# An adaptive-layernorm block on one core: the last four groups of tokens go through every expert, and the end is scheduled anew

## The chip, the core and the metric

The kernel runs on one NeuronCore of a Trainium2 chip. The metric is the device time of one execution in microseconds (us). The engines are TensorE (PE; its weight loads are listed apart as PEld), VectorE (DVE), ScalarE (ACT), GpSimd (POOL) and SyncE (SP), which here issues nearly all DMAs. Each engine works through its own list in order.

## The reference

Eight sequences `x` of 2048 tokens and 256 channels go through one block; all arithmetic is float32:

- six vectors per sequence (shift, scale and gate for each half) come from `silu(c) @ wmod`; the gates are kept away from zero;
- `h = layernorm(x) * (1 + ca) + sa`, then linear attention with 16 heads of 64 channels: queries and keys through `elu + 1`, a decay per token and head `a = sigmoid(h @ Wa + ba + 2)`, a running state `S = a S + k v^T` and a running sum `z = a z + k`, output `(q S) / (q z + eps)`, then `@ Wo`; `x = x + ga * that`;
- `h = layernorm(x) * (1 + cb) + sb`, then a mixture of 8 experts, each a 256 x 256 matrix with a bias: softmax of `h @ gate_W + gate_b`, the best two experts with their weights (at least 0.1 each, then scaled to a sum of one), `out = sum(weight * (h @ W_e + b_e)) / 2`; `x = x + gb * out`.

## The kernel before

**Groups and steps.** The tokens are cut into 64 groups of 256 (two chunks of 128), eight groups to a sequence. One loop over `n` from -2 to 64 (L1180) writes out the work of all engines by hand: in step `n` group `n` does its attention (`c0` and `c1`, the two chunks: scores, keys, values, outputs, state, project), group `n+1` its projections to queries and keys, running sums and denominators, group `n+2` its first norm and decays, group `n-1` (`prev`) its second norm and its routing. Generators (`routing`, `norm`, `project`, `chunk_decays`, ...) are moved on piece by piece by `advance`, so the order in the loop body is the order of each engine's list. Step 64 has no group of its own, only the norm and the routing of group 63; behind it comes a loop for what is left, the tail.

**Routed experts.** The groups of one unit (`UNITS`, L59: one sequence; the last sequence has a unit of four groups and one of two) scatter their normed rows, as they are routed, into a list per expert in DRAM (`xrows`, one indirect DMA of POOL for each chunk and choice). When the unit's last group is routed, `plan` turns the counts into a table of tiles of 128 rows. An `ExpertTile` then loads its rows `xg` and its expert's weights `we` (SP reads row and expert from the table into registers first), `turn`s the rows (two PE transposes, two ScalarE operations that apply shift and scale to `xgT`), and `apply`s them (four PE records `py`, one DVE sum with the bias, one store to `yrows`). At most four such tiles are on the chip (`AHEAD`), at most two turned. When all tiles of a unit are done, a `Combine` for each of its groups gathers the two results of every token (four indirect DMAs of POOL into `yc`), loads `x` again (`xc`, one buffer), weighs and adds (ScalarE, then DVE, then a multiply by the gate and an addition, L1032 and L1033), and stores.

**How many tiles where.** `share` holds five numbers for a step: so many tiles at its start, behind the second norm's transposes (L1260), behind the decays of the coming group (L1310), behind chunk 1's scores (L1346) and at its end (L1393). `expert_tiles(k, look)` turns one tile ahead of the one it applies; with `look` false the last one turns nothing ahead. In the last sequence (`late`, from step 57) the shares are `[1, 3, 3, 3, 2]`, `[0, 0, 0, 3, 2]` where a new unit has only been planned, and `[3, 2, 1, 0, 3]` in step 63.

**Dense experts.** The last two groups (`dense_from = total - 2`) are not scattered. All eight experts are applied to all their tokens: a `DenseTile` is one expert on one group, eight PE records that take the group's `h2T` as it stands and two DVE sums (L973) that weigh the product by `comb`, the matrix of weights with zeros for experts not chosen. The expert matrices are put over the query and key weights `wq_sb` and `wk_sb` once no projection is left, that is in step 63 (L1266 to L1275). `biases` (L917) starts the sums `acc`: `comb` is turned on PE, copied by DVE, multiplied by the biases on PE, copied by ScalarE. `finish` (L937) multiplies by the gate and adds to `xt` on DVE, then stores.

**The end.** Combines are fetched and finished once in the middle of a late step (L1291 to L1293) and once at its end (L1385, L1398). From step 64 on, three buffers that are free by then (`rooms`: dec, kT, qT) hold a whole combine each; those multiply and add on DVE, the others on POOL. In step 64 routed and dense tiles are mixed one by one (L1188 to L1194).

**Queues.** What a DMA on SP waits for holds everything behind it on SP: each routed tile puts a store, two register loads and two loads there, and the denominators (`rdd`, L474, then `rb`, L479), the decays (`dec` L419, `el` L409), the combines' `xc` and their stores stand in the same list. Indirect DMAs stand in POOL's list with its arithmetic.

## Time and profile before

| | |
|---|---|
| median of 14 runs | 3657.91 us (3651.53 to 3670.09) |
| profiled execution | 3657.18 us, span from first to last instruction 3655.5 us |
| granted TensorE clock, mean | 0.985 |
| PE busy | 3467.5 us, 95% of the span |
| DVE, ACT, POOL busy | 2760.2, 2068.4, 1897.0 us |
| chain that ended last | PE 64%, DVE 19%, DMA 7%, ACT 4% |
| DMA | 712.11 MB, mean 195 GB/s |
| routed tiles | 311 (`we` loads) |
| gathers and scatters | 248 gathers for 62 combines, 248 + 72 scatters |

The page's strip divides the span into 40 slices and gives the busy share of each engine in tenths; the windows view gives busy time, granted clock and DMA share in a stretch that one names; the waits view lists who waited for whom; the timeline has the instructions in order. A routed tile shows as four records of L900 (`py`) behind two of L884 (`pxt`), a dense one as eight of L966 (`py_d`).

### The profile page before, as it was taken

To read this page: it belongs to the slowest core of one execution; us is meant where nothing else is said; L and a number is where in the kernel's file an instruction comes from. 1 tells how busy PE (TensorE), PEld (TensorE's weight loads), DVE (VectorE), ACT (ScalarE), POOL (GpSimd) and SP (SyncE) were. 2 spreads that over 40 slices of the span, in tenths; PEclk is the share of its full clock that TensorE was granted. 3 is DMA by queue.
4 is the path that set the end of the run, shared out by engine and by line. 5 is a ranking of instruction groups with operands and counts; after the bars stand their busy time and mean duration, and the time that the engine had idled before them with its cause. 6 is when DMAs were issued, how large, how long until landed. Compare 5 with 4: busy or idle time off the path is not lost.

```text
span 3655.5 us, 82235 instructions
## 1 busy us (share of the span) xinstructions
PE 3467.5 (95%) x28998; PEld 2676.3 (73%) x28998; DVE 2760.2 (76%) x6395; ACT 2068.4 (57%) x5295; POOL 1897.0 (52%) x2114
## 2 busy tenths in 40 slices
PE   8999999999999999999999999999999999989886
PEld 6777767777777777777777777777777777666665
DVE  5777787887787777787777778777788777767755
ACT  5555555565566565566556555556656556555532
POOL 3444453443655556555565556555465555555654
PEclk9999999999999999999999999999999999999988
DMA  6555447656667767767776766766766776777866
GB/s 171 148 161 149 127 147 203 182 168 189 194 194 216 210 178 218 206 193 205 196 209 197 226 189 186 232 182 195 222 186 197 222 197 182 226 215 225 235 210 206
DMA packets 347406, 712.11 MB, mean 195 GB/s; under 512 B 43736, under 2 KB 212968, under 8 KB 322416
## 3 DMA queue, kind: packets, MB, share of 16 engines
q1 hardware_dynamic: 318880, 631.29, 60.9%
q0 software_dynamic: 27264, 74.49, 6.0%
q8 instruction: 229, 3.75, 0.4%
q14 instruction: 185, 1.52, 0.1%
q10 hardware_dynamic: 848, 1.07, 0.1%
HBM read 577.29 MB, written 132.53 MB: 194 GB/s over the span
## 4 chain that ended last, share of the span: by engine, by line
PE 64%; DVE 19%; DMA 7%; ACT 4%; issue 3%; SPq 1%; POOL 1%; DVEq 0%; POOLq 0%; ACTq 0%
PE pv L542 11%; PE pw L629 9%; PE pk L340 9%; PE po L579 6%; PE pq L340 6%; PE py L900 6%; DVE at L447 5%; PE sc L506 4%; PE po L562 3%; DMA rb<-rdd 3%; PE ps L613 3%; DVE qT L352 2%; PE pxt L884 2%; PE pk L525 2%; DVE dec L515 2%
## 5 line engine op out<-in xcount | busy, mean ns | idle before, releaser
L429 ACT ACTIVATE dec<-dec,lt 128x128 f32<-128x128 f32 x2048 | 628.7, 389 | 20.3 <-POOL dec L423 20.2
L1177 POOL TENSOR_TENSOR at<-at,qT 128x512 f32<-128x512 f32 x256 | 341.8, 1347 | 414.0 <-DVE qT L352 334.3
L542 PE MATMUL pv<-wv_sb,hT_a 128*128 128x512 f32 x1024 | 487.9, 609 | 25.7 <-DVE kd L528 23.1
L340 PE MATMUL pk<-hT_a,wk_sb 128*128 128x256 f32 x2048 | 503.3, 391 | 0.0
L340 PE MATMUL pq<-hT_a,wq_sb 128*128 128x256 f32 x2048 | 485.4, 385 | 2.3 <-DVE yg L904 1.2
L629 PE MATMUL pw<-wo_sb,oT 128*128 128x256 f32 x2048 | 470.1, 383 | 6.3 <-DMA el<-led 4.7
L889 ACT ACTIVATE xgT<-pxt,modT,modT 128x128 f32<-128x128 f32 x622 | 247.3, 448 | 393.1 <-PE pxt L884 392.6
L629 PEld LDWEIGHTS pw<-wo_sb,oT 128*128 128x128 f32 x2048 | 387.5, 192 | 58.0 <-DVE oT L591 7.6
L340 PEld LDWEIGHTS pk<-hT_a,wk_sb 128*128 128x128 f32 x2048 | 377.6, 194 | 59.6 <-DVE dx L633 6.7
L340 PEld LDWEIGHTS pq<-hT_a,wq_sb 128*128 128x128 f32 x2048 | 379.1, 190 | 55.5 <-ACT xgT L889 2.2
L447 DVE TENSOR_TENSOR_SCAN at<-at,z,kT 128x256 f32<-128x256 f32 x448 | 406.8, 948 | 2.0
L423 POOL TENSOR_SCALAR_AFFINE_SELECT dec<-dec 128x2048 f32<-128x2048 f32 x128 | 261.9, 2046 | 272.8 <-DMA dec<-led 159.3
L515 DVE TENSOR_TENSOR dec<-sc,dec 128x512 f32<-128x512 f32 x512 | 326.9, 681 | 42.3 <-PE sc L506 42.3
L900 PE MATMUL py<-we,xgT 128*128 128x256 f32 x1244 | 339.6, 398 | 17.7 <-ACT xgT L889 8.3
L542 PEld LDWEIGHTS pv<-wv_sb,hT_a 128*128 128x128 f32 x1024 | 186.1, 192 | 226.9 <-issue 164.8
L591 DVE TENSOR_TENSOR oT<-po,rb 128x512 f32<-128x512 f32 x256 | 168.7, 685 | 206.9 <-DMA rb<-rdd 114.4
L506 PE MATMUL sc<-qT,kT 64*128 64x128 f32 x4096 | 295.7, 284 | 0.0
L634 POOL TENSOR_TENSOR xt<-xt,dx 128x256 f32<-128x256 f32 x128 | 93.5, 730 | 388.0 <-DVE dx L633 386.1
L506 PEld LDWEIGHTS sc<-qT,kT 64*128 64x128 f32 x4096 | 248.3, 187 | 62.3 <-issue 62.3
L350 ACT ACTIVATE lowq<-pq 128x512 f32<-128x512 f32 x256 | 152.8, 597 | 246.7 <-PE pq L340 146.2
L1062 POOL TENSOR_TENSOR el<-el,qT 128x1024 f32<-128x1024 f32 x120 | 287.1, 2392 | 5.6 <-POOL whole L1070 0.2
L549 ACT COPY v<-pv 128x512 f32<-128x512 f32 x256 | 146.9, 580 | 252.8 <-PE pv L542 252.8
(198 smaller groups left out, 6269.3 us busy)
## 6 DMA issues: line engine op xcount, KB each, us to landing
dec<-led SPq DMA_DIRECT2D x128, 1024.0 KB
we<-ew_d SPq DMA_DIRECT2D x311, 384.0 KB
at<-ad SPq DMA_DIRECT2D x128, 512.0 KB
el<-led SPq DMA_DIRECT2D x256, 256.0 KB
rb<-rdd SPq DMA_DIRECT2D x128, 512.0 KB
xg<-xrows SPq DMA_DIRECT2D x311, 128.0 KB
yrows<-yg SPq DMA_DIRECT2D x311, 128.0 KB
xt<-in_L_attn_x_dram SPq DMA_DIRECT2D x64, 256.0 KB
```

Of the source, the lines that this page charges most:

```text
L340: nc.tensor.matmul(pp[:, j * GT : (j + 1) * GT], w[:, k, (jj + j) * P : (jj + j + 1) * P], hT[:, k, :], start=(k == 0), stop=(k == KD - 1),)
L423: nc.gpsimd.affine_select(out=dec, in_=dec, compare_op=ALU.is_ge, fill=1e30, base=0, pattern=[[0, H], [1, C]], channel_multiplier=-1,)
L429: nc.scalar.activation(dec[:, h, :], dec[:, h, :], AF.Exp, scale=-1.0, bias=x.lt[:, 0, ch, h : h + 1])
L447: nc.vector.tensor_tensor_scan(zz[:, j, :], at[:, j, :], kT[:, j, :], 0.0 if z is None else z[:, j : j + 1], ALU.mult, ALU.add,)
L506: nc.tensor.matmul(sc[q][:, i, :], self.kT[rows, half * 4 + i, self.tok], self.qT[rows, half * 4 + i, self.tok], start=True, stop=True,)
L515: nc.vector.tensor_mul(w4, sc[q], w4)
L542: nc.tensor.matmul(pv, self.hT[:, k, self.tok], wv_sb[:, k, i * 512 : (i + 1) * 512], start=(k == 0), stop=(k == KD - 1),)
L629: nc.tensor.matmul(pw[:, :D], self.oT[:, j, :], wo_sb[:, j, :], start=(j == 0), stop=(j == NP - 1))
L889: nc.scalar.activation(self.xT[:, k, :], pt[:, k * P : (k + 1) * P], AF.Identity, bias=modT[3][:, k, b : b + 1], scale=modT[4][:, k, b : b ...
L900: nc.tensor.matmul(py[:, :D], self.xT[:, k, :], self.w[:, k, :], start=(k == 0), stop=(k == KD - 1))
L1062: nc.gpsimd.tensor_mul(el, el, x.qT[:, :, ch * C : (ch + 1) * C])
L1177: nc.gpsimd.tensor_mul(zz[:, part, :], zz[:, part, :], ahead.qT[:, part, :])
```

## The change

- The unit of the last sequence's groups 4 and 5 is dropped, and `dense_from` becomes `total - 4`: groups 60 to 63 are dense. `h2T` gets four buffers, `comb` too; the sums of four groups fill the tile that held those of two and the biases' matrix, so that matrix moves to a buffer of its own.
- Since the expert matrices can be loaded only in step 63, the dense groups are collected (`dense_units`) and started by `start_dense`: two in the middle of step 63, where the load of the table of tiles stood, the third ahead of that step's last share, the fourth in the middle of step 64. `biases` is cut in two, `turn_weights` and `biases`, and leaves `routing`; for several groups all are turned first.
- The late shares become `[1, 3, 1, 3, 3]`, in step 63 `[1, 3, 3, 3, 3]` and in step 64 `[5, 2, 3, 3, 2]`, with the first of step 64 behind the second norm's first half and two single tiles between the pieces of the last routing. In late steps the turn ahead of the third share is left out, and that share's last tile turns nothing ahead.
- From step 61 a third combine is finished and fetched in each step, behind the fourth share (`finish_outputs`, `fetch_outputs(False)`, a further `fetch_x`).
- All combines multiply and add on GpSimd. In the tail a combine is finished when four tiles have passed since it was fetched (`age`).

```diff
@@ -56,7 +56,7 @@
     NG = N // GT
 
 
-    UNITS = [(b, 0, NG) for b in range(B - 1)] + [(B - 1, 0, NG - 4), (B - 1, NG - 4, NG - 2)]
+    UNITS = [(b, 0, NG) for b in range(B - 1)] + [(B - 1, 0, NG - 4)]
 
     def tiles_of(unit):
         return (TOP_K * GT * (unit[2] - unit[1]) + E * (P - 1)) // P
@@ -316,7 +316,7 @@
                     ident,
                 )
         hT = wk2.tile(
-            [P, KD, GT], F32, tag=f"hT{shift}", name=f"hT_{tag}", bufs=2 if shift else 3
+            [P, KD, GT], F32, tag=f"hT{shift}", name=f"hT_{tag}", bufs=4 if shift else 3
         )
         for half in range(KD):
             nc.scalar.activation(
@@ -693,10 +693,6 @@
             nc.vector.tensor_mul(comb, picks[:, :, 0, :], wide(top[:, :, 0:1]))
             nc.vector.tensor_mul(mark, picks[:, :, 1, :], wide(top[:, :, 1:2]))
             nc.vector.tensor_add(comb, comb, mark)
-            yield
-            yield
-            yield
-            unit.biases()
             yield
             return
 
@@ -912,21 +908,27 @@
 
         def __init__(self, x):
             self.x, self.n = x, f"d{x.tag}"
-            self.comb = wk2.tile([P, G, E], F32, tag="comb", name=f"comb_{x.tag}")
-
-        def biases(self):
-
+            self.comb = wk2.tile([P, G, E], F32, tag="comb", name=f"comb_{x.tag}", bufs=4)
+
+        def turn_weights(self):
             pt = small_tile(f"pct_{self.n}")
             for ch in range(G):
                 nc.tensor.transpose(pt[:E, ch * P : (ch + 1) * P], self.comb[:, ch, :], ident)
-            turned = wk2.tile([P, GT], F32, tag="rd", name=f"combT_{self.n}", bufs=1)
-            nc.vector.tensor_copy(turned[:E], pt[:E, :GT])
+            part = self.x.n - dense_from
+            self.turned = wk2.tile(
+                [P, GT], F32, tag=("rd", "lnn")[part > 0], name=f"combT_{self.n}", bufs=(1, 6)[part > 0]
+            )
+            nc.vector.tensor_copy(self.turned[:E], pt[:E, :GT])
+
+        def biases(self):
+
+            turned = self.turned
             pb = small_tile(f"pb_{self.n}")
             for ch in range(G):
                 nc.tensor.matmul(
                     pb[:, ch * D : (ch + 1) * D],
                     turned[:E, ch * P : (ch + 1) * P],
-                    sums[:E, 2 * G, :],
+                    expert_b_sb[:E, :D],
                     start=True,
                     stop=True,
                 )
@@ -988,7 +990,8 @@
         def load(self, room=None):
 
             u = self.unit
-            self.engine = nc.vector if room else nc.gpsimd
+            self.room, self.age = room, 0
+            self.engine = nc.gpsimd
             if room:
                 hold = wk2.tile([P, 4 * TOP_K, D], F32, tag=room, name=f"xyc_{self.tag}")
                 self.x = hold[:, G * TOP_K : G * TOP_K + G, :]
@@ -1081,7 +1084,8 @@
     for n, (b, first, end) in enumerate(UNITS):
         for g in range(first, end):
             unit_of[b * NG + g] = n
-    dense_from = total - 2
+    dense_from = total - 4
+    dense_units = []
     def rest(gen):
 
         for got in gen:
@@ -1162,7 +1166,7 @@
             no_x.pop(0).load_x()
 
     def finish_outputs():
-        while len(fetched) > (2 if rooms else 0):
+        while fetched and len(fetched) > (2 if fetched[0].room else 0):
             fetched.pop(0).finish()
 
     def keep_sums(jj):
@@ -1175,6 +1179,16 @@
         if ahead:
             part = slice(2 * jj, 2 * jj + 2)
             nc.gpsimd.tensor_mul(zz[:, part, :], zz[:, part, :], ahead.qT[:, part, :])
+
+    def start_dense(some):
+
+        for u in some:
+            u.turn_weights()
+        for u in some:
+            u.biases()
+            queue.extend(DenseTile(u, e) for e in range(E))
+            left[u.n] = E
+            dense_units.remove(u)
 
     c0 = plan = planned = None
     for n in range(-2, total + 1):
@@ -1195,7 +1209,7 @@
 
         todo = len(queue) + len(loaded) + len(turned)
         if late and (todo or not planned):
-            share = [1, 3, 3, 3, 2]
+            share = [1, 3, 1, 3, 3] if here else [5, 2, 3, 3, 2]
         elif planned:
             share = [0, 0, 0, 3, 2] if late else [0, 0, 0, 2, 2]
         else:
@@ -1204,16 +1218,19 @@
                 -(-todo * (i + 1) // (5 * steps)) + (-todo * i // (5 * steps)) for i in range(5)
             ]
         if n == total - 1:
-            share = [3, 2, 1, 0, 3]
+            share = [1,3,3,3,3]
         own = here.dk if here else None
         if here:
             c0.scores(0)
             c0.keys()
             c0.scores(1)
-        expert_tiles(share[0], not late or n == total)
+        if here:
+            expert_tiles(share[0], not late)
         if prev:
             nf = norm(prev.xt, "f", prev.tag)
         advance(nf, 2)
+        if not here:
+            expert_tiles(share[0])
         if here:
             c0.values(0)
             c0.values(1)
@@ -1259,11 +1276,12 @@
         fetch_x()
         expert_tiles(share[1])
         if prev:
-            if n - 1 == dense_from:
+            if n == total - 1:
 
                 sums = wk2.tile([P, NP, GT], F32, tag="at", name="sums", bufs=1)
-                nc.sync.dma_start(out=sums[:E, 2 * G, :], in_=expert_b)
-            if n - 1 == dense_from:
+                expert_b_sb = wk2.tile([P, 2 * GT], F32, tag="low", name="expert_b_sb", bufs=2)
+                nc.sync.dma_start(out=expert_b_sb[:E, :D], in_=expert_b)
+            if n == total - 1:
 
                 for e in range(0, E, 4):
                     for k in range(KD):
@@ -1275,6 +1293,7 @@
                         )
             if n - 1 >= dense_from:
                 unit = DenseUnit(prev)
+                dense_units.append(unit)
             else:
                 u = unit_of[n - 1]
                 if units[u] is None:
@@ -1284,7 +1303,11 @@
         advance(rt)
         if coming:
             coming.hT = modulated(arows, coming.b, 0, 1, f"a{coming.tag}")
+        if n == total:
+            expert_tiles(1)
         advance(rt)
+        if n == total:
+            expert_tiles(1)
         advance(own, 2)
         if here:
             c0.project()
@@ -1296,7 +1319,7 @@
         advance(da)
         advance(zk)
         advance(kp)
-        if share[2]:
+        if share[2] and not late:
             turn_tile()
         advance(kp)
         advance(rt)
@@ -1307,7 +1330,7 @@
         if n == -1:
             gate_rows()
             gates_of[0] = gates(0)
-        expert_tiles(share[2])
+        expert_tiles(share[2], not late or not here)
         advance(dk)
         advance(zk)
         if ahead:
@@ -1333,9 +1356,8 @@
             planned = None
             for _ in range(AHEAD):
                 load_tile()
-        if prev and unit.dense:
-            queue.extend(DenseTile(unit, e) for e in range(E))
-            left[unit.n] = E
+        if n >= total - 1:
+            start_dense(dense_units[:2])
         advance(dk, 2)
         fetch_x()
         if here:
@@ -1344,6 +1366,9 @@
             c1.scores(1)
         advance(rt)
         expert_tiles(share[3])
+        if n > dense_from:
+            finish_outputs()
+            fetch_outputs(False)
         advance(dk)
         if not here:
             if ahead:
@@ -1368,6 +1393,7 @@
         advance(rt)
         advance(na)
         advance(dk)
+        fetch_x()
         if ahead:
             whole_decay(ahead, 0)
             decayed_queries(ahead, 0)
@@ -1390,6 +1416,8 @@
                 gates_of[ahead.b], f"{ahead.tag}_0",
             )
             c0.decay_state()
+        if n >= total - 1:
+            start_dense(dense_units[:])
         expert_tiles(share[4])
         if na is not None:
             arows = next(na)
@@ -1416,7 +1444,11 @@
     fetch_x()
     while queue or loaded or turned:
         expert_tiles(1)
-        finish_outputs()
+
+        for o in fetched:
+            o.age += 1
+        if fetched and fetched[0].age > 3:
+            fetched.pop(0).finish()
         fetch_outputs()
     while waiting or fetched:
         fetch_outputs()
```

## The prediction

> **What bounds the kernel now.** I read the page first, then busy time by step, then what TensorE (PE) waits for in the last steps, then the last 15 us in order of time. A step's end is taken at its second dx (L633), the last vector operation of chunk 1.
>
> From the page:
> ```profile
> PE 3467.5 (95%) x28998; PEld 2676.3 (73%) x28998; DVE 2760.2 (76%) x6395; ACT 2068.4 (57%) x5295; POOL 1897.0 (52%) x2114
> ...
> PE   8999999999999999999999999999999999989886
> ```
> PE is the bound except in the last four slices. The same by step: 54 (an ordinary one), then 57 to 63, then 64 with the tail (columns: PE, weight loads, DVE, ACT, POOL, granted clock, DMA share, GB/s).
> ```profile
> 2949.00:3002.80 53.80, 52.97 (x462) 41.28 (x462) 40.73 (x97) 32.47 (x83) 29.33 (x33) 1.00 0.71 204
> 3107.50:3169.10 61.60, 55.54 (x464) 42.61 (x466) 49.82 (x115) 32.93 (x85) 39.64 (x50) 0.97 0.68 201
> 3169.10:3240.00 70.90, 64.27 (x504) 48.72 (x504) 47.91 (x106) 38.48 (x99) 37.00 (x41) 0.98 0.80 233
> 3240.00:3313.40 73.40, 64.88 (x504) 49.39 (x504) 48.35 (x105) 38.70 (x99) 36.56 (x41) 0.95 0.81 225
> 3313.40:3380.70 67.30, 60.08 (x493) 45.79 (x494) 48.69 (x107) 36.20 (x93) 36.17 (x39) 1.00 0.79 224
> 3380.70:3442.60 61.90, 55.85 (x464) 42.61 (x464) 45.65 (x108) 32.69 (x83) 48.71 (x59) 0.97 0.73 211
> 3442.60:3509.30 66.70, 60.87 (x492) 46.84 (x492) 45.67 (x95) 34.70 (x87) 37.83 (x40) 1.00 0.82 247
> 3509.30:3572.10 62.80, 47.76 (x352) 36.25 (x352) 27.16 (x82) 18.60 (x50) 28.40 (x37) 0.81 0.64 193
> 3572.10:3655.50 83.40, 50.52 (x216) 40.06 (x216) 50.98 (x137) 20.21 (x48) 38.82 (x41) 0.84 0.70 216
> ```
> An ordinary step leaves PE idle 0.8 us, steps 57 to 62 six to nine each, step 63 15.0, the last stretch 32.9 at a clock of 0.84. What PE waits for in steps 58 to 62, and in step 63:
> ```profile
> PE pxt L884 <- DMA xg<-xrows: 18.9, 13, 4.9
> ```
> ```profile
> PE pxt L884 <- DMA xg<-xrows: 8.9, 1, 8.9
> PE py L900 <- ACT xgT L889: 3.0, 2, 2.6
> PE pb_d L926 <- DVE combT_d L923: 2.9, 1, 2.9
> ```
> Expert rows that have not landed. All engines' waits from 3572 on, first and second longest, then the timeline's last dense tiles and last operation:
> ```profile
> ACT xyc L1028 <- DMA xyc<-yrows,rows: 24.8, 10, 5.6
> POOL yc L1032 <- DMA we<-ew_d: 17.5, 1, 17.5
> ```
> ```profile
> 3637.47 7.17 PE L966 MATMUL py_d<-wk_sb,hT_f 128*128 128x256 f32 x32 [1.41 <-DVE sums L973]
> ...
> 3651.59 0.42 DVE L1033 TENSOR_TENSOR xyc<-xyc 128x256 f32<-128x256 f32 x1
> ```
> ScalarE waits for gathers, turns expert tiles late, and PE waits for those; behind PE's last matmul (3644.6) come 11 us of combining.
>
> **Unit prices.** A dense tile is 8 records: 7.17/4 = 1.79 us of PE. Two routed tiles lie between 3503.45 (first transpose) and 3505.68 (next project): 1.1 us each, but also two register loads and three DMAs on SP (3.6 us a tile without waits: xg issued at 3495.4, 3499.0, 3502.7). A gather costs POOL 1.26 us from start to start.
>
> **The balance.** Removed: 15 routed tiles (16.5 us PE, 54 us of SP), two combines (8 gathers), the ranks, plan and 16 scatters of the ninth unit. Added: 16 dense tiles (28.6 us PE) and two more bias sets (transposes 0.38, matmuls 1.13: 3.0 together). PE gets 15 us more work, so any gain must come out of waits. All 32 dense tiles must run after step 63 has overwritten the query and key weights.
>
> **Tiles by step**, counted from the shares. Before, steps 57 to 63: 5, 12, 12, 10, 5, 12, 9 routed, then 12 routed and 16 dense. After: 5, 11, 11, 11, 1+6, 11, then 6 routed and 6 dense (3+3), then 17 dense (shares 5, 2, 3, 3, 2 and two singles), and 9 in the tail. Steps 57 to 62 hold 56 tiles either way.
>
> **Steps 57 to 62.** The share after the decays falls from 3 to 1, without its turn ahead, and the last share rises from 2 to 3.
> - Gone: the waits at that place, 3.14 (3198.7), 4.89 (3269.9), 2.54 (3343.8) and 0.88 us (3471.6): 11.5. Half-clock stretches of 3.4 and 6.8 us follow the first two; half of them is lost, some 4.5 where PE works. In step 61, with group 60 dense, prank's wait for hist (1.47) and one behind qT (1.13) go: 2.6. Together 18.5.
> - Added: no turned tile is left for the fourth share; where that is so now (3150.0, 3423.6) PE waits 1.40 and 1.23 for ScalarE. Four steps by 1.3: 5.2. The third tile of the last share needs a load issued some 3 us earlier; loads take 2.4 to 8.5 us from issue to PE's release here, so 0 to 3 a step, middle 1.5: 6.
> - A third combine a step from 61: one more finish (ACT 2 x 0.49, DVE 2 x 0.48, POOL 2 x (0.89 + 0.72), one store and one load on SP) and four gathers, 5.0 us of POOL, in place of 5.1 us of scatters that dense groups lack. Its finish follows some 10 us behind its gathers, which take 5.0 and land 2.7 to 8.9 us after issue. ScalarE queues in order: behind its wait stand the last share's turns, then PE; DVE's sums stand behind ScalarE. Steps 61 and 62, 0 to 4.5 each with clock: 6. The store waits for POOL on SP ahead of rdd, but rdd now goes 3.7 us after rd; inside that I cost it nothing; uncovered, it delays rb by the same.
> - Sum 17.2 - 18.5 = -1.3, from -13 (only the 5.2 is paid) to +15 (11.5 gained; 5.2, 12 and 9 paid).
>
> **Step 63.** Three routed tiles fewer (-3.3), six dense (+10.7), two bias sets (+3.0). The first share falls from 3 to 1, so the 8.9 us wait goes, with 1.7 of half clock. Dense weights, 2 MB issued at 3540.5, are used now only at 3584; soon they are needed some 12 us after issue. At this step's 193 GB/s they take 10.9: wait 0 to 5, take 1. Sums behind an unlanded gather: 0 to 3, take 1. The combT wait stays. Sum +1.8, from -3 to +8.
>
> **Step 64 and the tail.** No DMA feeds PE here any more.
> - PE: 26 x 1.79 = 46.5; norm's transposes 1.2, gate 1.0, bias 1.5: 50.2.
> - Waits. Norm's second half stands on DVE behind the sums of five dense tiles: 0.5 + four small operations 0.8 + ACT 1.1 + handovers 0.3 = 2.7 (now 3.6). combT 0.6 to 2.9: 1.2. Matmuls behind DVE's sums 0 to 4.3 (now 4.3 with eight combines on DVE): 1.5.
> - Clock. Gaps of 2.40 (3127.1) and 1.80 us (3400.3) were followed by 3.4 us at 0.50; one of 2.54 (3343.8) was not. Two stretches: 0 to 6, take 3.
> - End: last matmul 3644.64 to last store of the dense finish 3646.78, and 3.46 from the last store to the end of the span: 5.6.
> - Combines: backlog gone, four left (before: nine in this stretch). POOL's sums are finished three to five tiles ahead of the end: nothing. Uncovered, 3.2 us on POOL against 1.7 on DVE for the last one.
> - Sum 64.2 against 83.4: -19.2, from -27 (all waits zero) to -11.
>
> **Two rules set against rows.** The Trainium skill, "GPSIMD Engine Reference", section Key points, says that VectorE is about twice as fast in elementwise work, which speaks against the move of the sums. The rows agree (multiply 0.89 and 0.42 us), and paid in full on three combines it would make the sum 4.5 us worse; the cover decides. "TensorE: Matmul & The Clock Gate", section What's actually happening, lets the clock fall after at least one idle window of about 3.4 us. By it none of my waits would cost clock, and the sum would be 3 us better; the rows after 1.80 and 2.40 decide against it.
>
> **Forecast.** The profiled execution is 3657.2 us with a span of 3655.5; the median, 3657.9, differs by less than the runs do among themselves. 3657.2 - 1.3 + 1.8 - 19.2 = 3638.5; I say 3638.
>
> **Rivals.**
> - *The spreading pays in full and the end closes tight*: -13, -1, -24: 3619. For it: the waits for rows are the largest item of PE in these steps. Against: no more than four tiles are on chip either way, so a wait may only move.
> - *The late steps take it back*: +10 and +6 against -19: 3654. For it: ScalarE and DVE queue in order behind gathers in steps 61 to 63. Against: only three steps.
> - *Dense sums or weights bound the end*: DVE has 52 sums by 0.48 = 25 us, norm and routing 7, finishes 6.8, combines 3.8, 43 of 64 us in order; if its pieces fall badly the gain is 7: 3650.
> - *Slower: SP's queue behind rb.* The third tile of the last share puts yrows, xg and we behind rb, where each tile holds SP for 5.7 to 8.3 us (yrows at 3242.2, 3250.5, 3256.2), ahead of the next chunk's dec and el. If steps 58 to 63 lengthen by 7 each, 42 - 19: 3680. It decides from (19 + 7)/6 = 4.4 us a step. Against: POOL's mask waits only 1.9 us for dec over steps 58 to 60.
>
> **Chances.** Forecast 0.50, spreading in full 0.22, taken back 0.12, end bound 0.08, SP 0.08. About 0.2% (7.3 us) is what can be told from no change. Faster takes in the first two, half of the end's case and a sixth of the third: 0.78; same 0.14; slower 0.08. The likeliest case alone reaches from 3626 to 3650; for eight in ten the range goes from the first rival's 3616 (its 3619 with the clock's 3) to 3656.
>
> **What would show it.** Right: the last stretch about 64 us with dense matmuls nearly without gaps, no waits for xg at the third share, last operation a dense xt add. Wrong: PE waits for xgT behind yc in steps 61 and 62; dense matmuls waiting for wq_sb; combines after the last matmul. The forecast fails if steps 57 to 63 change by more than 12 us in sum, or if the clock of the last stretch stays at 0.84.

## The result, and the profile after

The changed kernel takes 3692.04 us (median of 9 runs, 3684.16 to 3697.36) against 3658.47 us for the kernel before (43 runs, 3646.5 to 3671.78): a ratio of 1.0088, 95% interval 1.0075 to 1.0100. It is 33.6 us slower, where 20 us faster was forecast. Its profiled execution took 3702.28 us with a span of 3700.6; the granted clock is 0.982.

From the page of the changed kernel, busy time and PE's strip in 40 slices:

```profile
PE 3496.1 (94%) x29038; PEld 2700.0 (73%) x29038; DVE 2771.5 (75%) x6355; ACT 2053.5 (55%) x5263; POOL 1887.7 (51%) x2098
...
PE   8999999999999999999999999999999999887788
```

The last slice is better than before (8 for 6), but of the five ahead of it two are at 7 and three at 8, where two were at 9 and three at 8. By step, cut at the second dx as in the prediction: 57 to 63, then step 64 with the tail (columns: PE, weight loads, DVE, ACT, POOL, granted clock, DMA share, GB/s).

```profile
3121.50:3182.90 61.40, 56.55 (x464) 43.53 (x466) 50.15 (x115) 33.03 (x85) 39.66 (x50) 0.94 0.68 200
3182.90:3252.20 69.30, 62.24 (x498) 47.94 (x499) 47.94 (x105) 37.84 (x97) 36.98 (x41) 0.98 0.82 235
3252.20:3329.00 76.80, 64.00 (x498) 50.38 (x498) 45.80 (x104) 37.40 (x97) 36.54 (x40) 0.93 0.70 197
3329.00:3409.30 80.30, 65.26 (x500) 51.24 (x502) 46.55 (x108) 37.41 (x97) 36.51 (x40) 0.89 0.72 203
3409.30:3493.40 84.10, 63.29 (x470) 48.55 (x472) 51.52 (x108) 33.84 (x87) 47.97 (x56) 0.88 0.66 185
3493.40:3563.00 69.60, 60.01 (x480) 46.66 (x480) 42.67 (x88) 34.36 (x87) 40.08 (x40) 0.98 0.71 211
3563.00:3637.40 74.40, 58.62 (x394) 45.58 (x394) 30.19 (x77) 17.45 (x46) 26.67 (x29) 0.84 0.46 142
3637.40:3700.60 63.20, 51.50 (x226) 42.88 (x225) 43.11 (x111) 7.04 (x16) 28.59 (x33) 0.94 0.27 83
```

| stretch | before | after | difference | predicted |
|---|---|---|---|---|
| steps 57 to 62 | 401.8 | 441.5 | +39.7 | -1.3 (-13 to +15) |
| step 63 | 62.8 | 74.4 | +11.6 | +1.8 (-3 to +8) |
| step 64 and tail | 83.4 | 63.2 | -20.2 | -19.2 (-27 to -11) |

These add up to +31.1. The two spans differ by 45.1; the other 14.0 lie in the steps before 57, whose order the change leaves alone, and a second profile of the changed kernel (below) does not have them: its step 57 begins at 3106.8, that of the profile before at 3107.5. This start moves by as much without any change: in a second profile of the kernel before it is 3118.7.

So the end did what was predicted, and two and a half times its gain (51.3 us) was lost ahead of it, in steps 59 to 61 above all (+3.4, +13.0 and +22.2) with the clock at 0.93, 0.89 and 0.88.

**What the late steps wait for.** The longest waits of three engines in steps 58 to 62 of the changed kernel, the share that a cause has, its count and its longest:

```profile
ACT lny_f L288 <- DVE mv_f L284: 83.4, 5, 20.5
...
DVE yg L900 <- DMA yrows<-yg: 30.2, 4, 11.6
...
PE po L579 <- ACT v L549: 27.5, 4, 10.3
```

None of the three is in the prediction. The second does not exist before: in these steps DVE there waits for a product of an expert (`PE py`) ahead of its sum, never for a store. One place shows how they hang together, the turn from step 58 to step 59 of the changed kernel in order of time (in brackets the idle time ahead of an instruction, and what ended it):

```profile
3243.32 1.11 SPq L409 DMA_DIRECT2D at<-ad  x2
...
3244.53 0.54 SPq L419 DMA_DIRECT2D dec<-led  x1
...
3246.23 1.27 SPq L479 DMA_DIRECT2D rb<-rdd  x2
...
3247.39 0.75 DVE L900 TENSOR_TENSOR yg<-py,we 128x256 f32<-128x256 f32 x2
...
3247.56 1.83 SPq L409 DMA_DIRECT2D el<-led  x2
...
3248.72 0.42 DVE L900 TENSOR_TENSOR yg<-py,we 128x256 f32<-128x256 f32 x1 [0.58 <-PE py L896]
...
3250.89 0.41 SPq L901 DMA_DIRECT2D yrows<-yg  x1
...
3265.78 0.42 DVE L900 TENSOR_TENSOR yg<-py,we 128x256 f32<-128x256 f32 x1 [8.78 <-DMA yrows<-yg]
...
3267.32 0.29 ACT L288 ACTIVATE lny_f<-mv_f,eps_ln 128x2 f32<-128x2 f32 x1 [17.70 <-DVE mv_f L284]
...
3267.76 1.05 ACT L549 COPY v<-pv 128x512 f32<-128x512 f32 x2
...
3268.38 0.91 PE L579 MATMUL po<-dec,v 128*64 128x128 f32 x6 [7.51 <-ACT v L549]
```

Read from the bottom. PE stands 7.5 us because the copy of `v` is late; ScalarE copies `v` late because in its order the square root of the second norm comes first, and that waits for the statistics on DVE; DVE is late because it stands at an expert's sum whose result buffer is not free. The results of routed tiles live in `yg`, which has three buffers:

```
YG = 3                                                        # line 25
y = wk2.tile([P, D], F32, tag="yg", name=f"yg_{self.tag}", bufs=YG)   # in ExpertTile.apply
```

The changed shares put three tiles at a step's end (share[4], 3) and one at the next step's start (share[0], 1): four sums in a row. The fourth must wait until the store of the first has landed. That store was issued at 3250.89, and DVE goes on at 3265.78, 14.9 us later. The reason for the 15 us is shown only in part. SP had issued `at`, `dec`, `rb`, `el` and an output ahead of it, by the transfer view 1 MB, 1 MB, 1 MB, 0.5 MB and 0.25 MB within 7.6 us. By the same view 1.9 MB moved in these 7.6 us (3243.3 to 3250.9) and 4.17 MB, at 280 GB/s, from there to the release. So at least 2 MB still stood ahead of the store when it was issued, which is 7 us of the 14.9 at that rate; the other half, in which two loads of rows, two of weights and four gathers were issued too, stays open. Before, with shares of 2 and 1 there, three sums in a row met three buffers.

PE's gaps of this kind are 7.51 (3260.9), 10.35 (3337.7), 7.90 (3418.0), 1.76 (3502.1) and 3.70 us (3571.7), one at the start of each step from 59 to 63.

**Step 63 and the end.** PE's waits of the changed kernel in step 63, then those from 3637.4 on:

```profile
PE pb_d L928 <- DVE combT_d L921: 9.5, 2, 5.3
PE po L579 <- ACT v L549: 3.7, 1, 3.7
PE py L896 <- ACT xgT L885: 2.6, 1, 2.6
```
```profile
PE py_d L968 <- DVE sums L975: 3.0, 1, 3.0
PE pn_f L313 <- ACT lnn_f L302: 1.9, 1, 1.9
PE pb_d L928 <- DVE combT_d L921: 0.5, 1, 0.5
```

In step 63 the matrix of weights, turned by PE and copied by DVE just ahead of its use, is late twice (before: once, 2.9 us). In the last stretch the chain of work that ended last ends in a long run of dense products, and the timeline closes with POOL's last sum and the last dense addition:

```profile
3669.87 24.46 PE py_d L968 x112
```
```profile
3695.51 0.78 POOL L1036 TENSOR_TENSOR xyc<-xyc 128x256 f32<-128x256 f32 x1
3695.74 0.83 DVE L944 TENSOR_TENSOR xt<-xt,sums 128x256 f32<-128x256 f32 x1
...
3696.49 0.41 DVE L943 TENSOR_TENSOR sums<-sums,gt 128x256 f32<-128x256 f32 x1
...
3696.94 0.42 DVE L944 TENSOR_TENSOR xt<-xt,sums 128x256 f32<-128x256 f32 x1
```

### The profile page after: what moved, and what is told of

Read it like the earlier page. It is cut to its first block, busy times and chain, and to the rows that moved or that the text cites. A ratio compares the mean times of both kernels' runs of the same rounds, so it can differ in the third digit from the quotient of the medians.

```text
span 3700.6 us, 81954 instructions
## 1 busy us (share of the span) xinstructions
PE 3496.1 (94%) x29038; PEld 2700.0 (73%) x29038; DVE 2771.5 (75%) x6355; ACT 2053.5 (55%) x5263; POOL 1887.7 (51%) x2098
## 3 DMA queue, kind: packets, MB, share of 16 engines
q1 hardware_dynamic: 311344, 620.41, 59.5%
q8 instruction: 229, 3.75, 0.4%
## 4 chain that ended last, share of the span: by engine, by line
PE 60%; DVE 19%; DMA 8%; ACT 5%; issue 5%; POOL 2%; SPq 1%; DVEq 0%; POOLq 0%; ACTq 0%
PE pv L542 10%; PE pw L629 8%; PE pk L340 8%; PE po L579 6%; PE pq L340 5%; DVE at L447 5%; PE py L896 5%; PE sc L506 4%; PE po L562 3%; PE ps L613 3%; DMA yrows<-yg 2%; DVE qT L352 2%; ACT dec L429 2%; DMA rb<-rdd 2%; PE pk L525 2%
## 5 line engine op out<-in xcount | busy, mean ns | idle before, releaser
L340 PE MATMUL pq<-hT_a,wq_sb 128*128 128x256 f32 x2048 | 494.4, 391 | 3.4 <-DVE kT L352 3.2
L340 PEld LDWEIGHTS pq<-hT_a,wq_sb 128*128 128x128 f32 x2048 | 385.3, 193 | 60.8 <-DVE kT L352 5.3
L885 ACT ACTIVATE xgT<-pxt,modT,modT 128x128 f32<-128x128 f32 x592 | 234.5, 448 | 345.5 <-PE pxt L880 345.1
L896 PE MATMUL py<-we,xgT 128*128 128x256 f32 x1184 | 322.9, 397 | 31.1 <-ACT xgT L885 18.8
L506 PEld LDWEIGHTS sc<-qT,kT 64*128 64x128 f32 x4096 | 250.7, 189 | 62.8 <-issue 62.6
L579 PE MATMUL po<-dec,v 128*64 128x128 f32 x4096 | 259.7, 280 | 32.4 <-ACT v L549 31.4
```

The lines of the kernel that those rows point to most:

```text
L340: nc.tensor.matmul(pp[:, j * GT : (j + 1) * GT], w[:, k, (jj + j) * P : (jj + j + 1) * P], hT[:, k, :], start=(k == 0), stop=(k == KD - 1),)
L506: nc.tensor.matmul(sc[q][:, i, :], self.kT[rows, half * 4 + i, self.tok], self.qT[rows, half * 4 + i, self.tok], start=True, stop=True,)
L579: nc.tensor.matmul(po[half * DH : (half + 1) * DH, i, :], self.v[:, h * DH : (h + 1) * DH], self.dec[:, q * NP + j, :], start=(self.S is N ...
L896: nc.tensor.matmul(py[:, :D], self.xT[:, k, :], self.w[:, k, :], start=(k == 0), stop=(k == KD - 1))
```

## The experiments

The theory (A): the loss is that of four results in a row against three buffers, and through it of DVE, ScalarE, PE and the clock. The rival (B): the shares as such, three tiles at a step's end, cost the time by what they put on SP, whatever the number of buffers; later, what the third combine and the dense groups in step 63 put ahead of PE. The record has four chip numbers for the experiments (none for the result above), and they fall into two speeds. On chip 11 the kernel before takes 3661 us, as in the result (3658); on chips 10, 7 and 0 it takes 3805, 3800 and 3802, with every ordinary step some 3 us longer. Ratios are always to the kernel before on the same chip; durations of steps are compared at one speed, on one chip where that is said, and ratios of different chips are not subtracted from each other. The kernel before has no profile on a slower chip.

| kernel | chip | median us | ratio, 95% | 57 to 62 | 63 | 64, tail |
|---|---|---|---|---|---|---|
| before, second profile (one run) | 11 | 3666.98 | | 401.6 | 60.8 | 84.2 |
| after, second time | 11 | 3695.71 | 1.0092, 1.0062 to 1.0122 | 445.8 | 77.6 | 63.1 |
| fourth buffer, turned early | 11 | 3645.76 | 0.9958, 0.9943 to 0.9973 | 417.4 | 53.9 | 63.1 |
| fourth buffer, two combines | 11 | 3656.52 | 0.9984, 0.9969 to 1.0000 | 400.8 | 63.6 | 77.3 |
| before with the new shares | 10 | 3840.53 | 1.0096, 1.0071 to 1.0121 | 444.5 | 63.6 | 90.0 |
| fourth buffer | 10 | 3788.32 | 0.9956, 0.9938 to 0.9974 | 415.3 | 70.3 | 65.8 |
| fourth buffer, again | 7 | 3787.33 | 0.9960, 0.9943 to 0.9978 | 416.7 | 71.5 | 65.8 |
| old shares | 10 | 3782.21 | 0.9948, 0.9924 to 0.9972 | 416.3 | 72.1 | 65.8 |
| three in a row, three buffers | 7 | 3777.75 | 0.9958, 0.9938 to 0.9979 | 401.0 | 67.8 | 68.1 |
| third combine from 62 | 7 | 3777.70 | 0.9943, 0.9909 to 0.9977 | 415.4 | 55.1 | 77.0 |
| the same with the old shares | 7 | 3774.67 | 0.9926, 0.9896 to 0.9956 | 406.4 | 57.8 | 76.4 |
| third combine from 62, end's sums on VectorE | 0 | 3785.03 | 0.9953, 0.9937 to 0.9969 | 415.1 | 55.7 | 76.5 |

**1. A fourth result buffer.** The changed kernel with one number altered.

```diff
-YG = 3
+YG = 4
```

> The changed kernel with four instead of three buffers for the results of routed tiles (yg), nothing else. Theory A (the fourth tile in a row, three at a step's end and one at the next start, needs the yg buffer whose store stands on SyncE behind rb and el; VectorE waits there, with the second norm, ScalarE's copies of v and TensorE's outputs behind it): VectorE's wait of yg for yrows, 30 us in the four steps from 58 on and 5 in step 63, goes, TensorE's wait of po for v (27.5 in those steps) with it, and the time falls from 3692 by 25 to 35 to about 3662. Rival B (the third tile behind rb fills SyncE's list and delays dec, el and xg whatever buffers there are): the waits of POOL for el and of TensorE for xg remain, gain under 8 us. Rival C (routing and ScalarE's turns have lost the matmuls that covered them when the third share went from 3 to 1): gain under 10 us, waits for xgT and hist stay.

Measured: 0.9956 (0.9938 to 0.9974). One buffer turns a slower kernel into a faster one, by ratios from different chips (the changed kernel itself was not timed on chip 10). DVE's wait for the store of `yg` is gone from the list of steps 58 to 62, and PE's for `v` with it; what is left there is what rivals B and C named, PE's waits for rows (13.4 us) and for `xgT` (11.2). Of the last five steps only 61 (74.5) and 63 (70.3) stay long; step 63 keeps its two waits for the turned weights, 9.6 us.

**2. The old shares in the changed kernel.** Three buffers, but two tiles at a step's end, as before.

```diff
-            share = [1, 3, 1, 3, 3] if here else [5, 2, 3, 3, 2]
+            share = [1, 3, 3, 3, 2] if here else [5, 2, 3, 3, 2]
...
-        if share[2] and not late:
+        if share[2]:
             turn_tile()
...
-        expert_tiles(share[2], not late or not here)
+        expert_tiles(share[2])
```

> The changed kernel with the late shares of before, 1, 3, 3, 3, 2, and the turn ahead at the third share, three yg buffers; steps 63 and 64 keep their new shares, the four dense groups and the third combine stay. Theory A, and C too: steps 58 to 61 go back to near what they were before (273 us, against 310 in the changed kernel's profile), the last stretch keeps its gain of 20 us, step 63 loses about 5 of the 12 it had grown: 3692 - 35 - 5, about 3650, a little faster than before. Rival D (the third combine and the dense groups' bias sets in steps 61 to 63 are what costs): step 61 stays above 78 us and the time above 3675.

Measured: 0.9948 (0.9924 to 0.9972). Taking the shares back cures the kernel as well as the buffer does, and by as much as can be told. All the rest of the change (dense groups, third combine, the new shares of steps 63 and 64, the new end) is then worth half a per cent on this chip.

**3. The new shares in the kernel before.** The reverse: nothing of the change but the distribution.

```diff
-            share = [1, 3, 3, 3, 2]
+            share = [1, 3, 1, 3, 3] if here else [1, 3, 3, 3, 2]
...
-        if share[2]:
+        if share[2] and not late:
             turn_tile()
...
-        expert_tiles(share[2])
+        expert_tiles(share[2], not late or not here)
```

> The kernel before with the new late shares alone, 1, 3, 1, 3, 3 and no turn ahead at the third; step 63 keeps 3, 2, 1, 0, 3, the last stretch its shares, two groups dense. Theory A: the wait of yg for yrows appears in each of steps 58 to 62 with 8 to 11 us and the time rises by 30 to 45 us, to about 3695; step 63, where the first share is 3, can add more. Rival D: no more than 10 us above before.

Measured: 1.0096 (1.0071 to 1.0121), the size of the whole loss. The waits of DVE in steps 58 to 62 of this kernel have the line that the kernel before lacks:

```profile
DVE yg L904 <- DMA yrows<-yg: 42.3, 4, 11.4
```

Steps 59 to 62 take 80.0, 80.1, 78.0 and 75.3 us. Shares alone make the loss; dense groups and combines are not needed for it.

**4. The changed kernel and the kernel before, once more.** Is the wait there in every profile of the one and in none of the other?

> The changed kernel itself, beside the next three on one chip, since this chip may stand otherwise to the first one than the three experiments so far: a ratio of about 1.009 to the kernel before if a share of the time is lost to VectorE's wait for yrows, whose length goes with the transfers.

> The kernel before, for its profile on this chip: the steps 57 to 64 to compare the others with. VectorE does not wait of yg for yrows in steps 58 to 62, since three tiles in a row have three buffers.

Measured: 1.0092 (1.0062 to 1.0122) for the changed kernel, and in its second profile, DVE in steps 58 to 62:

```profile
DVE yg L900 <- DMA yrows<-yg: 37.1, 4, 11.0
```

The steps from 57 on take 61.6, 66.9, 79.1, 80.0, 84.8, 73.4 and 77.6 us, and the last stretch 63.1. The kernel before has no such wait in its second profile either: 60.9, 70.0, 71.1, 69.2, 63.2, 67.2, 60.8 and 84.2. What is read from one profile of each holds.

**5. Fourth buffer, and no third combine.** What is left of the late steps, 61 above all?

```diff
-YG = 3
+YG = 4
...
-        if n > dense_from:
+        if n >= total:
             finish_outputs()
             fetch_outputs(False)
```

> Four yg buffers, and the third finish and fetch of combines only in step 64, not in steps 61 to 63. My prediction charged the third combine 6 us in steps 61 and 62 (ScalarE waits for gathers, TensorE for xgT behind it) and 1 in step 63: those steps get 7 us shorter against four buffers alone, the last stretch, with three more combines to gather and finish, 0 to 5 longer. Against that: if ScalarE's waits for gathers only move to the other fetches, no difference of more than 3.

Measured: 0.9984 (0.9969 to 1.0000). Step 61 and the last stretch by the windows:

```profile
3383.00:3447.20 64.20, 57.23 (x471) 43.91 (x471) 44.53 (x105) 33.56 (x85) 42.16 (x48) 0.97 0.76 221
3575.20:3652.50 77.30, 52.91 (x226) 43.73 (x225) 47.98 (x117) 10.09 (x22) 49.54 (x57) 0.83 0.36 109
```

Steps 57 to 62 take 400.8 us, what the kernel before takes (401.6), so without the run against three buffers and without the third combine nothing is lost there. But the three combines left out of steps 61 to 63 come back at the end: 28 gathers instead of 16 in the last stretch, POOL at 49.5 us instead of 28.6, and 77.3 us instead of 63.1, a loss far above the 0 to 5 expected. PE's last matmul ends at 3634.0, and POOL is still adding 15.0 us later:

```profile
3648.27 0.72 POOL L1036 TENSOR_TENSOR xyc<-xyc 128x256 f32<-128x256 f32 x1
```

In the changed kernel that distance is 2.0 us (3694.3 to 3696.3).

**6. Fourth buffer, weights turned early.** The third combine stays; each dense group's weights are turned and copied inside its routing, two pieces behind `comb`, and not just ahead of the biases.

```diff
-YG = 3
+YG = 4
...
             nc.vector.tensor_add(comb, comb, mark)
             yield
+            yield
+            unit.turn_weights()
+            yield
             return
...
         def turn_weights(self):
+            if self.turned is not None:
+                return
...
-            part = self.x.n - dense_from
-            self.turned = wk2.tile(
-                [P, GT], F32, tag=("rd", "lnn")[part > 0], name=f"combT_{self.n}", bufs=(1, 6)[part > 0]
-            )
+            self.turned = wk2.tile([P, GT], F32, tag="lnn", name=f"combT_{self.n}", bufs=6)
```

> Four yg buffers, and the weights of groups 60 to 62 are turned and copied in the step in which they are routed, behind chunk 1's scores, so that step 63 only multiplies them by the biases. Theory: in step 63 TensorE waits 4.2 and 5.3 us for the copies (combT) since they queue on VectorE behind its other work; with the half clock that follows, step 63 gets 10 us shorter than with four buffers alone (70). Rival: TensorE then waits at the same place for something else (the weights of the experts, still landing, or VectorE's sums): under 4 us.

Measured: 0.9958 (0.9943 to 0.9973), 3645.76 us. Steps 61 and 63 and the last stretch:

```profile
3381.40:3459.70 78.30, 63.66 (x472) 48.28 (x472) 53.21 (x108) 34.17 (x87) 47.96 (x56) 0.87 0.73 200
3525.80:3579.70 53.90, 48.84 (x389) 37.71 (x390) 30.60 (x75) 17.76 (x46) 27.84 (x31) 1.00 0.67 203
3579.70:3642.80 63.10, 50.25 (x227) 42.16 (x225) 43.01 (x111) 7.05 (x16) 28.58 (x33) 0.96 0.28 84
```

Step 63 falls from 77.6 (experiment 4, same chip) to 53.9 us, with no wait for `combT` and the clock at 1.00 instead of 0.80 (in that profile; 0.84 in the first one of the changed kernel); a part of that is the buffer's, since the wait for `v` at its start is gone too. Step 61 stays long; its waits on ScalarE and on PE are those that the prediction named for the third combine:

```profile
ACT yc L1033 <- DMA yc<-yrows,rows: 7.7, 2, 5.8
```
```profile
PE py L899 <- ACT xgT L888: 5.6, 1, 5.6
```

With experiments 4 to 6, all on chip 11, steps 57 to 62 come apart: 445.8 as changed, 417.4 with the fourth buffer and the early turning (-28.4), 400.8 with the fourth buffer, no third combine and no early turning (-16.6, of which 14.1 in step 61). The turning touches steps 61 and 62 only. In steps 57 to 60 the buffer alone gives 287.6 against 273.0 (-14.6); the 13.8 of steps 61 and 62, and the 16.6, hold a share of the turning that was not measured apart. PE's waits in step 61 of this kernel put 0.4 us to it and 5.6 to `xgT`.

**7. Three in a row, three buffers.** Theory A says that it is the run of four against three that costs; then the shares may keep three tiles at the end, if none follows at the start. Rival B holds the three at the end to be the cost. The same tiles a step up to step 62, other places, and one tile fewer in step 63; run beside the fourth buffer.

```diff
-            share = [1, 3, 1, 3, 3] if here else [5, 2, 3, 3, 2]
+            share = [0, 3, 2, 3, 3] if here else [5, 2, 3, 3, 2]
...
-            share = [1,3,3,3,3]
+            share = [0, 3, 3, 3, 3]
```

> The changed kernel with its three yg buffers, and late shares 0, 3, 2, 3, 3 (in step 63 0, 3, 3, 3, 3): the last share keeps its third tile behind rb, but no tile follows at the next step's start, so three results stand in a row. Theory A: VectorE's wait of yg for yrows at a step's start goes without a buffer more, and the time falls by some 30 us against the changed kernel, to a ratio of about 1.000 to 1.003. Rival B (the third tile behind rb fills SyncE's list): steps 58 to 61 stay near 310 us and the ratio at 1.007 or above.

> The changed kernel with four yg buffers once more, on the same chip as the next three, since its first measurement was on a chip where every step takes 3 us longer. Theory A (the fourth tile in a row lacks a buffer) gives a ratio of about 0.996 to the kernel before, against 1.009 for the changed kernel.

Measured: 0.9958 (0.9938 to 0.9979) and 0.9960 (0.9943 to 0.9978). Steps 58 to 60 in one window, for three in a row, for the fourth buffer, and for the kernel before with the new shares (experiment 3); the first two are on chip 7, the third on chip 10, of the same speed:

```profile
3299.90:3496.40 196.50, 181.69 (x1492) 140.26 (x1492) 139.14 (x315) 113.16 (x291) 112.98 (x121) 1.00 0.84 241
```
```profile
3295.80:3506.20 210.40, 188.35 (x1492) 146.34 (x1490) 134.34 (x315) 113.66 (x291) 110.66 (x121) 0.95 0.82 227
```
```profile
3309.30:3536.10 226.80, 190.25 (x1492) 148.28 (x1490) 138.31 (x315) 112.44 (x291) 109.74 (x121) 0.93 0.75 208
```

All three issue 1492 PE records and 315 on DVE. Three tiles at the end with three buffers cost nothing once the fourth is elsewhere: B falls. That these three steps are even 13.9 us shorter than with the fourth buffer was not expected, nor a ratio below 1.000. The clock is 1.00 against 0.95, PE waits 9.2 us for rows against 12.9, and DVE 8.3 us for `rb` against 15.7. Which of these is cause and which effect was not tried.

**8. The third combine from step 62 on.** Experiment 6 with the third combine left out of step 61, the step that suffers.

```diff
-        if n > dense_from:
+        if n > dense_from + 1:
             finish_outputs()
             fetch_outputs(False)
```

> Four yg buffers, combT turned early, and the third combine only from step 62 on. Step 61, where the plan of the last routed unit scatters too, took 78.3 us with the third combine and 64.2 without it; the last stretch took 63.1 with all and 77.3 without those of steps 61 to 63. Expected: step 61 falls by 10 to 14, the last stretch, with one combine more, grows by 2 to 5; ratio about 0.993. If the backlog of combines bounds the last stretch as soon as one is added, the two cancel and the ratio stays at 0.996.

Measured: 0.9943 (0.9909 to 0.9977). Against the fourth buffer of experiment 7, on the same chip, step 61 gains 5.6 us (74.6 to 69.0), step 63 16.4 (71.5 to 55.1, mostly the early turning), and the last stretch loses 11.2 (65.8 to 77.0). Step 61 gains less, and the last stretch loses more, than was expected. One combine more falls into that stretch, 20 gathers instead of 16. The loss has two pieces: PE's last matmul ends 67.0 us after the start of the stretch instead of 59.5, and 9.9 us ahead of its end instead of 6.3. For the first, the timeline shows a place:

```profile
3742.70 0.96 POOL L1009 DMA_INDIRECT xyc<-yrows,rows  x1 [0.30 <-issue]
3743.67 0.48 DVE L977 SCALAR_TENSOR_TENSOR sums<-py_d,comb,sums 128x256 f32<-128x256 f32 x1 [5.14 <-remote]
3744.20 2.07 PE L970 MATMUL py_d<-wk_sb,hT_f 128*128 128x256 f32 x4 [4.50 <-issue]
```

From 3723.7 to 3743.7 POOL issues 16 gathers back to back. A dense sum on DVE stands for 5.14 us and starts as the last of them is issued; PE, 4.5 us idle, follows it by half a microsecond, and the clock behind it is 0.74 from 3745 to 3760. What released that sum the profile does not name ("remote"), so its cause stays open.

**9. The same with the old shares.** Are old shares and fourth buffer of use together?

```diff
-            share = [1, 3, 1, 3, 3] if here else [5, 2, 3, 3, 2]
+            share = [1, 3, 3, 3, 2] if here else [5, 2, 3, 3, 2]
...
-        if share[2] and not late:
+        if share[2]:
             turn_tile()
...
-        expert_tiles(share[2], not late or not here)
+        expert_tiles(share[2])
```

> As the one before, with the late shares 1, 3, 3, 3, 2 and the turn ahead at the third share. My prediction made the new shares alone worth 1.3 us where nothing else waits: with a fourth buffer the difference between the two sets should be under 5 us, ratio within 0.0015 of the one before. Rival: spreading the tiles is worth its 11.5 us of waits for rows, and this is 10 us slower.

Measured: 0.9926 (0.9896 to 0.9956), the lowest of all, but its interval overlaps that of experiment 8, and the medians differ by 3.0 us, under the 5 expected; the rival, 10 us slower, falls. Steps 57 to 62 are 406.4 against 415.4, which speaks for the old shares even with four buffers.

**10. The end's sums on VectorE.** Experiment 8, with the combines that have a room multiplying and adding on DVE as before.

```diff
-            self.engine = nc.gpsimd
+            self.engine = nc.vector if room else nc.gpsimd
```

> As the kernel with four yg buffers, combT turned early and the third combine from step 62 on, with one edit: combines that lie in a whole free buffer multiply and add on VectorE again, as before the change. In that kernel's last stretch (77.0 us) the dense work is done and GpSimd then multiplies and adds for four combines, 13.4 us in a row, at the very end; in the changed kernel three combines end 1 us ahead of the dense groups. Theory: with VectorE's 1.7 us a combine against GpSimd's 3.3, and VectorE free by then, the last stretch falls to 66 to 70 and the ratio from 0.994 to about 0.992. Rival: the sums then stand ahead of dense sums on VectorE and hold TensorE: under 3 us.

Measured: 0.9953 (0.9937 to 0.9969), the last stretch 76.5 against 77.0 (chip 0 against chip 7, of the same speed). PE's dense products wait longer for DVE; first experiment 8, then this one, PE in the last stretch:

```profile
PE py_d L970 <- DVE sums L977: 5.3, 3, 3.0
```
```profile
PE py_d L970 <- DVE sums L977: 9.6, 4, 3.8
```

PE's last matmul ends 69.3 us after the start of the stretch (67.0 in experiment 8) and 7.2 us ahead of its end (9.9): what DVE gains behind the matmuls, it loses among them.

## Why the prediction was wrong, and where it was right

**Steps 57 to 62 (predicted -1.3, measured +39.7): the step that failed is "Added", its item on the last share's third tile.** It was costed by the load of the tile's rows alone, "0 to 3 a step, middle 1.5: 6". A tile also needs a result buffer, and a third one at a step's end together with the one at the next step's start makes a run of four against three buffers. That cost up to 28.4 us on chip 11 (experiments 4 and 6): 9.1 and 9.5 in steps 59 and 60, 6.5 and 7.4 in steps 61 and 62, where the early turning has a share, less 4.0 in the two ahead of them. In steps 58 to 62 the trace of before could not show the wait, since a run of three just fits; the code could: `YG` stands in line 25. One seam of the kernel before did hold more than three, two sums at the end of step 62 and three at the start of step 63, and its fourth sum came late:

```profile
3525.00 0.42 DVE L904 TENSOR_TENSOR yg<-py,we 128x256 f32<-128x256 f32 x1 [10.51 <-PE py L900]
```

The profile puts that wait down to the product, whose rows were late (the 8.9 us of PE that the prediction quotes). So it gave no sign of a missing buffer; whether the store would have held the sum too, it does not show.

**"Gone": it moved.** PE's wait for rows is 0.4 us in steps 57 to 62 of the changed kernel, but only while PE waits for the late `v` as well. With the fourth buffer and without the third combine (experiment 5) it is 12.5 us, against 18.9 and 12.6 in the two profiles of the kernel before: the waits behind the decays went, others came, some 12 us into steps 59 and 60 above all (3.23 and 2.72). That a wait "may only move" stands in the prediction, as the argument against its first rival; its forecast counted the 11.5 as gone all the same. PE's waits for `xgT`, costed at 5.2, rose by 6.4 (3.1 to 9.5). The balance came out inside the range nevertheless: without the third combine's 6 the prediction gives -1.3 - 6 = -7.3, and experiment 5 measured 400.8 against 401.6, -0.8. In neither list were two waits of PE for `hist` (`prank`) in steps 59 and 60, 4.8 us.

**The third combine ("steps 61 and 62 ...: 6"): mis-sized.** Experiments 5 and 6 give 16.6 for steps 57 to 62, 14.1 of it in step 61 alone, where POOL issues scatters as well; a share of this belongs to the early turning, by which the two differ too. The mechanism was the one named, PE behind `xgT` behind ScalarE's wait for `yc`. Leaving it out gains nothing in sum either: the last stretch then takes 14.2 us more (63.1 against 77.3).

**Step 63 (+1.8, measured +11.6): "The combT wait stays" is the term that failed.** Before it was one wait of 2.9 us; now PE waits twice, 4.21 us ahead of the biases of the first two groups (to 3598.2) and 5.28 ahead of the third's (to 3623.8), since the copies stand on DVE behind other work. That is 6.6 us more than before; the clock, 0.84, was no better before (0.81). Turned early the step takes 55.1 instead of 71.5 us (experiment 8 against the fourth buffer on the same chip). The 3.7 us for `v` at the step's start are the buffer's again. These two, 10.3 us, are about what the step took beyond the +1.8. The dense weights and the gathers, costed at 1 each, do not show among its waits.

**Step 64 and the tail (-19.2, measured -20.2): right, and by its terms.** 63.2 us against 64.2 predicted; PE 51.5 against 50.2; waits of 1.9 for the norm (2.7), 0.5 for combT (1.2), 3.0 for the sums (1.5); clock 0.94. That the three waits add up to the same 5.4 us as predicted is luck, since each is off by 0.7 us or more. The last operation is a dense `xt` addition, as it said. The cover was thinner than said: POOL's sums end at 3696.3, one us ahead of the dense finish and not three to five tiles.

**The two rules.** That VectorE is about twice as fast as GpSimd in elementwise work (the Trainium skill, "GPSIMD Engine Reference", Key points) agrees with the rows, 0.42 against 0.72 to 0.91 us, but using it gained nothing (experiment 10), where PE waited longer for DVE's sums (9.6 us against 5.3). The idle window of about 3.4 us that "TensorE: Matmul & The Clock Gate" (What's actually happening) asks for ahead of a slower clock is not borne out again: the changed kernel has a gap of 1.87 us at 3646.0, and by the windows

```profile
3648.30:3651.70 3.40, 3.35 (x10) 2.80 (x10) 0.48 (x1) 1.03 (x3) 0.00 (x0) 0.50 0.00 0
```

the clock is at half for the next 3.4 us with PE busy all through.

**The rivals.** The slower one had the place and the size, "the third tile of the last share" on SP, 7 us a step, and wanted 3680; its mechanism (`dec` and `el` delayed) was another than the one that came. Its chance of 0.08 was set by POOL's short waits for `dec`, which bear on that mechanism alone. Of "the late steps take it back" step 61 came true, without the size. That the spreading pays in full did not come in any profile on chip 11: there steps 57 to 62 never took less than 400.8 us, where this rival needed 389.

**A better version.** The fourth buffer with early turning takes 0.9958 of the time before on chip 11; on chip 7, the old shares with the fourth buffer, early turning and the third combine from step 62 take 0.9926 (0.9896 to 0.9956). Both beat the kernel before; the first beats the changed kernel too, on one chip (3645.76 against 3695.71 us). Three in a row with early turning was not tried.

## What to carry to other kernels

When work is moved between places in an order written by hand, count for each rotating buffer the longest run of producers between two points where it drains, across the seam of two iterations too, and hold it against the number of buffers; a run that just fits shows no wait in the trace and breaks with one more, and a longer run can stand behind another wait that carries its own name. A store is not done when it is issued: here it held its buffer for 14.9 us with other transfers ahead of it on the same queue, and DVE's wait for it came out as a wait of PE, two engines on. Deferred work off the critical path (the combines here) is a debt: price it where it will be paid, not only where it is taken away.

## What the runs showed of the hardware

- A store of 128 KB, issued on a queue that had been given 3.75 MB in the 7.6 us ahead of it, released its buffer 14.9 us after its issue (3250.89 to 3265.78).
- An addition on VectorE took twice as long beside GpSimd's additions. In the last lines of the changed kernel shown above, the same addition of two on-chip operands takes DVE 0.83 us while POOL adds (3695.74) and 0.42 us once POOL has ended (3696.94). The Trainium skill, "SBUF — State Buffer", section SBUF: two separate sides, has the two engines take turns at one pair of ports, the whole instruction long, where DVE reads two operands from there; the rows fit that roughly: POOL's addition ends at 3696.29, and 0.42 us later would be 3696.71, where DVE's ended at 3696.57. The prediction costed the end's DVE work without it.
- The same kernel takes 3.8 to 3.9% longer on chips 10, 7 and 0 (3800 to 3805 us) than on chip 11 (3661 us). Beyond the result, the changed kernel was timed on chip 11 alone, and the versions with only the fourth buffer, the old shares or three in a row on chips 10 and 7 alone; so by how much each of them beats the changed kernel on one chip is known only for the versions of experiments 5 and 6.
